# Fetching a block's neighbour lists by node in layer 0 of a two-layer graph attention kernel

## The chip, the core and the metric

The kernel runs on one core of a Trainium2 chip. The metric is the device time of one execution in microseconds. A core has five engines that each work through their own queue of instructions in order: TensorE (PE, matrix products), VectorE (DVE), ScalarE (ACT), GpSimd (POOL) and SyncE (SP). They wait for each other by semaphores. Transfers between the chip's memory and the on-chip buffer are done by 16 DMA engines. An indirect transfer, a gather of rows by a list of row numbers, is issued by POOL.

## What is computed

A graph of 2708 nodes goes through two layers of attention. Each node has 1024 features, and `adj` says which pairs are neighbours; a node has a few to 40 of them. The reference, cut to what matters:

```python
def layer0(x, adj):
    f = x @ Wf + bf
    g = x @ Wg + bg
    e = relu(f @ g.T)
    attention = softmax(where(adj > 0, e, -9e15), axis=1)
    return attention @ (x @ W + bW)

def layer1(x, adj):
    h = x @ W1
    e = leaky_relu(h @ a1 + (h @ a2).T, 0.2)
    attention = softmax(where(adj > 0, e, -9e15), axis=1)
    return relu(attention @ h)

x = layernorm(x + layer0(x, adj))
x = layernorm(x + layer1(x, adj))
```

## The kernel before

The kernel does not work on the 2708 x 2708 matrix. A prelude reads `adj` once and makes of each row a list of its neighbours' numbers, 40 places long (`CAP`), which goes to `LD` in the chip's memory (`keep_lists`, line 625). A list is stored as 4 runs of 10 places (`QT`), place t of run q being neighbour 4t + q. Nodes are then sorted by the length of their lists and cut into 85 groups of 32 nodes; four groups make a block of 128 rows, and there are 22 blocks (one of them has a single group).

A group is worked on as a set of tiles. A tile has 128 partitions: partition 32q + i stands for node i of the group, and holds one neighbour of that node, the t-th of run q. So the lists of a group are needed as a 128 x 10 piece of the buffer `SL`, whose partition 32q + i holds run q of node i. `SL` (line 152) is one tile of 128 x 85 x 10 integers for all groups. `load_lists(b)` (line 1065) fetches them: for each of the block's 4 groups it issues one gather of 128 short rows (10 integers, 40 bytes) out of `LD`, by the row numbers `idq`, straight into the group's piece of `SL`. Another table, `ids`, holds the number of the node in each of a block's 128 rows.

Layer 0 is a loop over the 22 blocks (the loop that calls `lay.sums` at line 1279). One round k, for block u, does in this order:

- `lay.sums` (line 920): PE multiplies the softmax weights of block u into the neighbours' rows of `x`, which lie in the `ring`, a buffer of 20 tiles of 128 rows with 4 KB each. Each time both halves of a tile are used up, its place is free, and `gathers` (line 877) issues on POOL the gather of the next tile into it: 128 rows of `x`, 512 KB, by one column of `SL`. A block has 20 tiles in most rounds, so these are the tiles of the next block.
- POOL's queue then gets: the scatter of the finished block before to `T1` (in `close`, line 1139), the gather of a later block's own rows (`load_x`, line 1087), the gather of the residual rows into `z` (`load_residual`, line 1133), and `load_lists` for the block four rounds on (line 1316). Rounds 1 to 17 have such a call.
- PE makes the two dense products of the round (f for the block two rounds on, the output product of the block before), ACT copies f to the partitions of the tiles (`replicate`).
- `dots` (line 1123): DVE makes one dot product per tile of the next block, as soon as that tile has landed. `soft` (line 1128) makes the softmax weights of the next block. The norm of the block before follows (`close`).

The class `InOrder` keeps each engine's instructions in the order in which the program issues them. The waits are put in by the recording layer, from what each instruction reads and writes. Each of POOL's DMAs adds 16 to one of eight semaphores, taken in turn, when all of its data has landed, and a DMA waits until the one before it on its semaphore has landed, eight DMAs back.

Layer 1 works on the same lists, all of which are in `SL` by then, and gathers from `T1`. All engine calls go through a helper, so every operation of both layers has the line number 71 in the profile.

Of the kernel before, what the change touches and what calls it, by code (L numbers as in the profile page):

```python
# [10 lines left out]
I32 = mybir.dt.int32  # L11
# [23 lines left out]
CAP = 40  # L35
# [71 lines left out]
def listed_path(ctx, tc, x, adj, Wf, bf, Wg, bg, W, bW, W1, a1, a2, out):  # L107

    nc = tc.nc
    P = 128  # L110
# [8 lines left out]
    nrows = [32] + [P] * (NB - 1)  # L119
    valid = [N - 32 * (NG - 1)] + [P] * (NB - 1)  # L120
    start = [0] + [valid[0] + P * b for b in range(NB - 1)]
    groups = [[0]] + [list(range(g, g + 4)) for g in range(1, NG, 4)]
    QT = CAP // 4
    Q = 4
# [8 lines left out]
    pe, dve, act, pool, sp = (InOrder(tc, e) for e in (nc.tensor, nc.vector, nc.scalar, nc.gpsimd, nc.sync))  # L133
# [8 lines left out]
    LD = dram.tile([N * Q, QT], I32, name="LD")  # L142
# [9 lines left out]
    SL = const.tile([P, NG, QT], I32, name="SL")  # L152
    SL0 = const.tile([P, NSL0, QT], I32, name="SL0")
    ids = const.tile([P, NB], I32, name="ids")
# [28 lines left out]
    def gather(engine, dst, table, idx, rows=N):  # L183
        engine.indirect_dma_start(
            out=dst, out_offset=None, in_=table,
            in_offset=bass.IndirectOffsetOnAxis(ap=idx, axis=0), bounds_check=rows - 1, oob_is_err=False)
# [33 lines left out]
    with ExitStack() as prelude:  # L220
        new_pool = lambda name, bufs: prelude.enter_context(tc.tile_pool(name=name, bufs=bufs))
# [476 lines left out]
        t = adjp.tile([P, N], F32, name="adj")  # L698
# [6 lines left out]
        b = full - 1  # L705
# [136 lines left out]
    def cut(most, turns, order):  # L842


        units, at = [], 0
        for i, b in enumerate(order):
            u = Unit()
            u.b, u.gs, u.at = b, groups[b], at
            u.G, u.T, u.n = len(u.gs), max(TILES[g] for g in u.gs), nrows[b]
            u.tiles = [(k, g, t) for k, g in enumerate(u.gs) for t in range(TILES[g])]  # L850
            u.col = {(k, t): m for m, (k, g, t) in enumerate(u.tiles)}
            u.tiles.sort(key=lambda m: (m[0] // turns, m[2]))
            u.sc = scores[i % 2][:, :u.G, :u.T]
            assert len(u.tiles) <= min(most, MOST)
            at += len(u.tiles)
            units.append(u)
        return units

    class Layer:
# [3 lines left out]
        def __init__(self, units, rings, width, table, stp):  # L863
            self.units, self.table, self.width, self.stp = units, table, width, stp

            self.first = {g: i for i, g in enumerate(g for u in units for g in u.gs)}
            self.slots = [(t, i) for t in rings for i in range(t.shape[1])]
            self.count = len(self.slots)
            self.order = [(u, g, t) for u in units for _, g, t in u.tiles]
            assert all(self.first[g] < NSL0 for _, g, _ in self.order[:self.count])  # L870
            self.next, self.free, self.most = 0, set(), len(self.order)

        def rows(self, m):
            t, k = self.slots[m % self.count]
            return t[:, k, :self.width]

        def gathers(self, latest=None):
            ready = []
            while self.next < min(self.most, len(self.order)) and (self.next < self.count or self.next - self.count in self.free):
                ready.append(self.next)  # L880
                self.next += 1
            if latest is not None and latest + self.count in ready:
                ready.remove(latest + self.count)
                ready.insert(0, latest + self.count)
            for m in ready:
                u, g, t = self.order[m]
                idx = SL[:, g, t:t + 1] if m >= self.count else SL0[:, self.first[g], t:t + 1]
                gather(pool, self.rows(m), self.table, idx)

        def soft(self, u):  # L890

# [173 lines left out]
    def load_lists(b):  # L1065
        for g in groups[b]:
            gather(pool, SL[:, g, :], LD[:, :], idq[:, g:g + 1], N * Q)

    def spread(v, n, name):

        qd = small.tile([P, Q], F32, name=name)
        dve.tensor_scalar(qd[:n], quad[:n], v, None, op0=ALU.mult)
        return qd
# [3 lines left out]
    with s0s:  # L1077
        new_pool = lambda name, bufs: s0s.enter_context(tc.tile_pool(name=name, bufs=bufs))
        tp, frp = new_pool("tp", 2), new_pool("frp", Q)
        stp, xp, yp, jp = (new_pool(n, 1) for n in ("stp0", "xp", "yp", "jp0"))  # L1080
        zs = new_pool("zp", 1).tile([P, TW], F32, name="z")
        seq = [1, 0, *range(2, NB)]
        units = cut(R0, 2, seq)
        lay = Layer(units, [ring], D, x, stp)
        xb, q, qd, F, Fr, xTs, yTs, Wp, y, Z = ({} for _ in range(10))
# [23 lines left out]
        def x_turn(b):  # L1109
            xTs[b] = tp.tile([P, KC, P], F32, name="xT")  # L1110
            for _ in turn(xb[b], nrows[b], xTs[b]):
                pass
# [4 lines left out]
        def replicate(b, k):  # L1117

            Fr[b, k] = frp.tile([P, D], F32, name="Fr")
            for p in range(Q):  # L1120
                act.copy(Fr[b, k][32 * p:32 * p + 32, :], flat(F[b])[32 * k:32 * k + 32, :])
# [130 lines left out]
        for k, u in enumerate(units):  # L1252
            nxt = units[k + 1] if k + 1 < len(units) else None
            b = u.b
            back = seq[k - 1] if k > 0 else None
            ahead = seq[k + 2] if k + 2 < NB else None

            first = k == 0
            po = ps_s.tile([P, H, 512], F32, name="po")
            y[b] = yp.tile([P, D], F32, name="y")  # L1260
            if back is not None:
                for _ in yTs[back][1]:
                    pass
            reps = list(range(len(nxt.gs))) if nxt is not None and not first else []
            for r in reps[:1]:
                replicate(nxt.b, r)
            next(closing, None)
            if loaded is not None:
                q_dot(loaded)
                loaded = None  # L1270
            next(closing, None)
            for r in reps[1:3]:
                replicate(nxt.b, r)
            if nxt is None:

                for _ in closing:
                    pass
                Wp[back] = product(P, yTs.pop(back)[0], Wt, 1)
            lay.sums(u, po, y[b])
            if first:  # L1280
                u_rows()
            for _ in closing:
                pass
            closing = iter(())
            if ahead is not None and not first:
                x_turn(ahead)
            if k + 3 < NB and not first:
                loaded = seq[k + 3]
                load_x(loaded)
            if back is not None and nxt is not None:  # L1290
                load_residual(back)
                if back > 0:
                    Wp[back] = product(P, yTs.pop(back)[0], Wt, 1)
                else:
                    Wp[back] = whole(split_product(yTs.pop(back)[0], Wt, frp.tile([P, D], F32, name="Fr"), 1))
            if k + 2 == NB:
                load_residual(b)
            spreading = iter(())
            if ahead is not None and not first:
                spreading = q_spread(ahead)  # L1300
                next(spreading)
            for r in reps[3:]:
                replicate(nxt.b, r)
            if ahead is not None and not first:
                f_product(ahead)
            if ahead == NB - 1:
                sp.dma_start(M, W1.rearrange("(k p) d -> p k d", p=P))
            yT = tp.tile([P, KC, P], F32, name="xT")
            steps = turn(y[b], nrows[b], yT, halves=True)
            next(steps)  # L1310
            yTs[b] = yT, steps
            if k + 2 == NB:
                for _ in steps:
                    pass
            if k + 4 < NB and not first:
                load_lists(seq[k + 4])
            if nxt is not None:
                dots(nxt, 0, len(nxt.tiles))
            for _ in spreading:
                pass  # L1320
            if nxt is not None:
                soft(nxt)
            if back is not None:
                closing = close(back)
                next(closing)
        b = NB - 1
# [10 lines left out]
    with ExitStack() as s1s:  # L1337
        new_pool = lambda name, bufs: s1s.enter_context(tc.tile_pool(name=name, bufs=bufs))
# [11 lines left out]
        lay = Halves(units, [ring, more], TW, T1[:, :], stp)  # L1350
        done1 = {b: i for i, b in enumerate(order1)}
        for u in units:
            g, at = u.gs[0], lay.first[u.gs[0]]
# [90 lines left out]
        for n, (u, ks) in enumerate(parts):  # L1444
            b, po = u.b, banks[:, n % 2, :]
# [7 lines left out]
            if turning is not None:  # L1453
                v, kv, _ = turning
# [11 lines left out]
            if ks[-1] + 1 == u.G:  # L1466
                k = done1[b]
# [387 lines left out]
```

## Time and profile before

| | |
|---|---|
| median of 9 runs | 1715.17 us (1712.06 to 1718.64) |
| the profiled execution | 1716.65 us; its span 1714.9 us, so 1.75 us lie around the span |
| busy in the span | PE 1540.4 us (90%), DVE 1291.9 (75%), ACT 631.3 (37%), POOL 1159.6 (68%) |
| the loop of layer 0 | about 240 to 1050 us after the span's start |
| gathers of tiles in layer 0 | 405, mean 1069 ns each on POOL |
| gathers of lists | 85, mean 1022 ns each on POOL; 68 of them in the loop, in 17 rounds |
| one round, scatter to `T1` to scatter to `T1` | 41.0 us, mean of the 15 from 319.25 to 934.42 us |

The busy time of a gather on POOL is the time in which POOL issues it. The data lands later; that is read from the start of the instruction that waits for it. Two gathers that follow each other directly start 1.29 us apart, 0.99 us of issuing and 0.30 us between. "Idle before" in a row is how long the engine stood still, and the arrow names what the profile takes to have ended that.

### The profile page before, as it was taken

Reading aid. Unit: us, or ns where it says so; the run is one execution under the profiler, and the core shown is the slowest. Engines: PE = TensorE matmul, PEld = TensorE weight load, DVE = VectorE, ACT = ScalarE, POOL = GpSimd, SP = SyncE. Lnnn points to the kernel's source line nnn. Section 1 sums busy time; section 2 is a strip of 40 time slices with the busy share of each in tenths; the row PEclk is TensorE's granted clock in tenths of the full one; section 3 lists DMA queues with packets and bytes.
Section 4 is the critical chain, followed back from the end, with each engine's and each line's share of the span. In section 5 each row is a group of like instructions: output and inputs, shape, how many; then the busy total and the mean of one; then the engine's idle time right before and its main releaser. Section 6 shows DMA issues by size and latency. Waiting matters only on the chain. (4 is left out here: it accounts for less than half of the span.)

```text
span 1714.9 us, 22758 instructions
## 1 busy us (share of the span) xinstructions
PE 1540.4 (90%) x6851; PEld 664.2 (39%) x6873; DVE 1291.9 (75%) x4158; ACT 631.3 (37%) x886; POOL 1159.6 (68%) x1130
## 2 busy tenths in 40 slices
PE   6996779899999999999999999379998988999896
PEld 3542333343444444444444444123333433334332
DVE  6998668898999988999999788456566555665662
ACT  6671425554554544444444554011111111111111
POOL 7994674667676766777667644377777777777740
PEclk9998989999999999999999999789999999999998
DMA  8772584777887877888877766599999999999961
GB/s 339 295 258 115 195 310 146 271 252 274 297 298 282 285 271 286 296 289 295 299 277 265 280 232 260 179 396 367 370 371 396 391 390 374 386 394 391 391 253 38
DMA packets 150961, 503.95 MB, mean 294 GB/s; under 512 B 32714, under 2 KB 32730, under 8 KB 148398
## 3 DMA queue, kind: packets, MB, share of 16 engines
q0 software_dynamic: 131648, 428.27, 67.7%
q1 hardware_dynamic: 16128, 73.71, 11.3%
q8 instruction: 56, 0.92, 0.2%
q10 hardware_dynamic: 3054, 0.43, 0.1%
q14 instruction: 75, 0.61, 0.1%
HBM read 510.81 MB, written 33.75 MB: 318 GB/s over the span
## 5 line engine op out<-in xcount | busy, mean ns | idle before, releaser
L71 POOL DMA_INDIRECT ring<-in_x_dram,SL x405 | 432.8, 1069 | 159.0 <-issue 76.2
L71 DVE SCALAR_TENSOR_TENSOR j<-ring,Fr 128x1024 bf16<-128x1024 f32 x402 | 493.2, 1227 | 54.9 <-ACT Fr L71 23.7
L71 PE MATMUL po<-ring,st 128*32 128x512 f32 x2616 | 330.0, 623 | 58.5 <-DVE st L71 28.0
L71 ACT COPY Fr<-pm 32x1024 f32<-32x1024 f32 (+2 forms) x353 | 340.6, 965 | 6.9 <-PE pm L71 2.1
L71 PE MATMUL pm<-M,yT 128*128 128x512 f32 (+1 forms) x704 | 313.3, 598 | 0.5 <-ACT yT L71 0.5
L71 POOL DMA_INDIRECT ring<-T,SL x249 | 246.9, 992 | 81.3 <-issue 66.2
L71 PE MATMUL pm<-Wt,xT 128*128 128x512 f32 (+1 forms) x704 | 297.0, 594 | 0.1
L71 PE MATMUL pm<-M,xT 128*128 128x512 f32 x672 | 295.0, 597 | 0.3 <-issue 0.2
L71 ACT ACTIVATE scores<-scores 128x12 f32<-128x12 f32 (+9 forms) x65 | 14.0, 216 | 641.9 <-DVE scores L71 641.9
L71 PEld LDWEIGHTS pm<-M,yT 128*128 128x128 f32 (+1 forms) x704 | 127.8, 186 | 184.7 <-issue 183.5
L71 PEld LDWEIGHTS pm<-Wt,xT 128*128 128x128 f32 (+1 forms) x704 | 129.6, 187 | 156.1 <-issue 152.2
L71 PEld LDWEIGHTS pm<-M,xT 128*128 128x128 f32 x672 | 128.9, 192 | 155.6 <-issue 152.6
L71 POOL DMA_INDIRECT more<-T,SL x156 | 154.6, 991 | 47.9 <-issue 42.5
L71 PEld LDWEIGHTS po<-ring,st 128*32 128x32 f32 x2616 | 95.5, 114 | 234.1 <-issue 160.7
L71 POOL TENSOR_TENSOR adj<-adj,iota 128x2708 f32<-128x2708 f32 (+2 forms) x23 | 124.5, 5458 | 11.6 <-ACT adj L71 11.6
L71 PE MATMUL pm<-halfT,Wt 128*128 128x512 f32 x256 | 118.9, 620 | 0.0
L71 DVE MAX8 cand<-adj 128x8 f32<-128x170 f32 x336 | 95.6, 321 | 17.9 <-POOL adj L71 17.9
L71 POOL DMA_INDIRECT SL<-LD,idq x85 | 86.8, 1022 | 28.1 <-issue 24.2
L71 PE MATMUL po<-more,st 128*32 128x512 f32 x624 | 86.6, 648 | 13.9 <-ACT y L71 13.9
L71 DVE TENSOR_SCALAR scores<-ring,f1q 128x4 f32<-128x4 f32 (+6 forms) x69 | 16.0, 238 | 94.3 <-DMA ring<-T,SL 71.4
L71 POOL DMA_INDIRECT z<-in_x_dram,ids x21 | 23.3, 1109 | 88.5 <-issue 31.9
L71 PEld LDWEIGHTS pm<-halfT,Wt 128*128 128x128 f32 x256 | 49.9, 200 | 59.2 <-issue 59.1
(236 smaller groups left out, 1466.7 us busy)
## 6 DMA issues: line engine op xcount, KB each, us to landing
adj<-in_adj_dram SPq DMA_DIRECT2D x19, 1354.0 KB, 7.0
X1S<-z SPq DMA_DIRECT2D x19, 512.0 KB, 5.9
ring<-in_x_dram,SL POOLq DMA_INDIRECT x405
rows<-in_L_gnn_Wg_dram SPq DMA_DIRECT2D x8, 512.0 KB
rows<-in_L_gnn_Wf_dram SPq DMA_DIRECT2D x8, 512.0 KB
M<-in_L_gnn_W_dram SPq DMA_DIRECT2D x1, 4096.0 KB
ring<-T,SL POOLq DMA_INDIRECT x249
u1b<-X1S SPq DMA_DIRECT2D x7, 512.0 KB, 4.9
```

The lines of the kernel that those rows point to most:

```text
L71: made = self.tc.keep_in_program_order(op(*args, **kwargs))
```

## The change

`load_lists` stays for the first blocks. In rounds 1 to 17 the call at line 1316 is replaced. `load_rows` issues one gather: for each of the block's 128 rows the whole list of its node (40 integers, 160 bytes), by `ids`, into a new tile `nodes` (two buffers). Partition 32k + i now holds all four runs of node i of group k. `place_rows` then copies 16 pieces of 32 x 10 integers on POOL, run q of group k to partitions 32q to 32q + 31 of the group's place in `SL`. It is a generator that does one copy at each step. `gathers` steps it once after each gather that it issues, so in the next round one copy stands in POOL's queue behind each of the first 16 gathers of tiles. What is left of it is done before the next `load_rows`.

```diff
             self.next, self.free, self.most = 0, set(), len(self.order)
+            self.between = iter(())
...
                 gather(pool, self.rows(m), self.table, idx)
+                next(self.between, None)
...
+    def load_rows(b, nodes):
+        t = nodes.tile([P, CAP], I32, name="nodes")
+        gather(pool, t[:nrows[b]], LD.rearrange("(n q) t -> n (q t)", q=Q), ids[:nrows[b], b:b + 1])
+        return t
+
+    def place_rows(b, t):
+        for k, g in enumerate(groups[b]):
+            for q in range(Q):
+                pool.tensor_copy(SL[32 * q:32 * q + 32, g, :], t[32 * k:32 * k + 32, q * QT:(q + 1) * QT])
+                yield
...
+        nodes = new_pool("nodes", 2)
...
+            for _ in lay.between:
+                pass
             if k + 4 < NB and not first:
-                load_lists(seq[k + 4])
+                lay.between = place_rows(seq[k + 4], load_rows(seq[k + 4], nodes))
```

## The prediction

> **What bounds the kernel now.** I read the busy time by stretches first, for four rounds of layer 0. The columns are the stretch, its length, then busy microseconds (and instructions) of PE, PE's weight loads, DVE, ACT and POOL, PE's granted clock, the DMA engines' share and GB/s.
>
> ```profile
> 575.00:616.00 41.00, 40.75 (x186) 17.74 (x186) 37.67 (x86) 20.76 (x25) 28.35 (x27) 1.00 0.78 271
> 616.00:658.00 42.00, 40.01 (x184) 17.44 (x184) 37.20 (x84) 20.77 (x25) 28.83 (x28) 1.00 0.76 270
> ```
>
> A round is full on PE (40.8 of 41 us) and nearly on DVE (37.7). POOL shows 28.4, but with the 0.30 us between gathers its 27 instructions take 27 x 1.29 = 35 us. All three are close to the bound. So little can be won here, and much be lost on any one of them. The timeline of POOL for the round from 607.93 us shows the rest (start, length, instruction, idle before):
>
> ```profile
> 607.93 1.02 POOL L71 DMA_INDIRECT T<-z,ids  x1 [0.30 <-DVE j L71]
> 609.25 1.03 POOL L71 DMA_INDIRECT xb<-in_x_dram,ids  x1 [0.30 <-issue]
> 615.15 0.99 POOL L71 DMA_INDIRECT z<-in_x_dram,ids  x1 [4.87 <-DVE scores L71]
> 616.45 1.00 POOL L71 DMA_INDIRECT SL<-LD,idq  x1 [0.30 <-issue]
> 617.75 1.21 POOL L71 DMA_INDIRECT SL<-LD,idq  x1 [0.30 <-issue]
> 619.26 1.00 POOL L71 DMA_INDIRECT SL<-LD,idq  x1 [0.30 <-issue]
> 620.57 0.99 POOL L71 DMA_INDIRECT SL<-LD,idq  x1 [0.30 <-issue]
> 621.87 1.00 POOL L71 DMA_INDIRECT ring<-in_x_dram,SL  x1 [0.30 <-issue]
> 623.17 0.99 POOL L71 DMA_INDIRECT ring<-in_x_dram,SL  x1 [0.30 <-DVE rstd L71]
> ...
> 648.13 0.99 POOL L71 DMA_INDIRECT ring<-in_x_dram,SL  x1 [0.30 <-issue]
> 649.42 1.01 POOL L71 DMA_INDIRECT T<-z,ids  x1 [0.30 <-issue]
> ```
>
> The 20 gathers of tiles take 27.55 us (621.87 to 649.42), one each 1.29 us or a little more, because none waits for the landing of the one before. The other part, scatter to first gather, takes 13.94. How long a gather of 512 KB takes to land is seen where DVE waits for `z` and finds the DMA queue otherwise short:
>
> ```profile
> 619.52 1.23 DVE L71 TENSOR_TENSOR z<-pm,z 128x1024 f32<-128x1024 f32 x1 [1.01 <-DMA z<-in_x_dram,ids]
> ```
>
> It was issued by 615.15 + 0.99 = 616.14 and used at 619.52: 3.38 us. Read in the same way, eight other rounds give 3.29 to 3.51. In the full stream it is longer: the fifth tile's gather ended at 628.76 and its dot product waited until 635.38, 6.6 us.
>
> **The change part by part.** *Removed:* three of the four list gathers, 3 x 1.30 = 3.9 us of POOL's queue in each of 17 rounds. They stand between `z` and the first tile, so the first tile can go 3.9 us earlier, if PE has a place free.
>
> *Added:* 16 copies of 32 x 10 integers on POOL per round. No row shows such a copy. The nearest are a POOL memset of 20 x 7 (104 ns) and the one POOL copy, 128 x 1 (371 ns); after a memset the next gather came 0.15 us later, after a gather 0.30. So copy and gap cost between 0.25 and 0.67 us, and I take 0.45, the middle, since its neighbours on both sides are equally far. The new tile costs nothing but buffer space. The one list gather left moves 128 rows of 160 bytes in place of 512 of 40, which only relieves the DMA queue.
>
> *Moved, and this decides:* a copy stands behind a gather, and it waits. I read the waits in the list of the changed program's instructions. In all 17 rounds it is the same. The first copy waits for the list gather. The second to fourth wait for no DMA. The fifth waits for everything POOL has issued up to then, tile gathers 1 to 5 with it, and each of the copies 6 to 16 waits for the semaphore value that the tile gather directly before it leaves: for its landing. Gathers 6 to 17 wait in turn for the copy before them. The cells of `SL` in question are not the same (the gathers read the next block's columns, the copies write a block three on), so it is an order that the data do not need, but the chip will keep it. So gathers 5 to 16 no longer stream. Each must land before the next is issued: 12 landings per round, 204 in all. Behind the waiting copy stand all later tile gathers, the scatter to `T1`, `xb` and `z`; DVE's dots and through them PE's sums wait for those.
>
> One such step is 0.99 (issue) + 3.37 (landing, the rows above, which fit since the queue now is short) + 0.45 = 4.81 us in place of 1.29. From the start of the 17th gather of one round to that of the next:
>
> - gathers 17 to 20, which have no copies: issued by 4.87, the last landed at 8.24;
> - its dot product, 1.27 from one to the next: 9.5; `soft` until PE starts its sums: 859.62 to 863.66 and 614.36 to 618.14 in two rounds, 3.9: 13.4; PE's first four matmuls, 0.46, and the semaphore: first place free at 14.0. POOL has its other work done at about 13.8 (scatter from 5.2, its landing some 5 us after 6.2 as at 568.61 to 573.87, then `z` and one list gather), so this is even;
> - four gathers with free copies, 4 x 1.45 = 5.8, and 0.5 for the first copy, whose list gather was issued just before: 20.3;
> - 12 steps of 4.81, 57.7: 78.0 us.
>
> Against 41.0 us this is +37.0 per round, and over 17 rounds +629. PE's dense work (28 us a round) and DVE's other work lie inside the 78 us and cost nothing; without this cover they would be the 41 us of now. Should PE's clock sag because it idles half the time (it shows 0.72 for 1100 to 1150 us, with PE 53% busy), only the 0.46 us before the first free place are on the path: 0.2 x 17 = 3 us. Nothing outside the loop changes. The sum is made against the profiled execution: 1716.65 + 629 = 2346, and as that execution lies 1.5 us above the median, 2345.
>
> Bounds of the step: 0.99 + 3.29 + 0.25 = 4.53 and 0.99 + 3.51 + 0.67 = 5.17. With the four free gathers at 1.25 and 1.66 and 0.2 to 1 for the first copy, the round is 73.6 or 83.7, the time 1715 + 17 x 32.6 = 2269 or 1715 + 17 x 42.7 = 2441.
>
> The Trainium skill prices a landing too ("DMA: Bandwidth & Descriptors", section "Anatomy of one DMA — SWDGE (gpsimd) path"): about 2.0 us plus bytes over 436 GB/s, nearly all of the fixed part being completion, which only a chain of dependent DMAs pays each time. For 512 KB that is 3.20 us, against the 3.38 of the row; by it the sum would be 204 x 0.17 = 35 us less, about 2310. It speaks against the change by the same mechanism.
>
> **The rivals.** *The landings cost what they cost in the full stream.* If the 6.6 us of the fifth tile's row were the latency of a scattered gather and not its queue, a step would be 8.04: 1715 + 17 x (37.0 + 12 x 3.23) = 3003. Against it: `z` is a gather of the same table by equally scattered rows, and lands in 3.3 to 3.5. Chance 0.04.
>
> *The waits are met early and only the copies count.* POOL's round gets 16 x 0.45 - 3.9 = 3.3 us longer, and as the tiles feed DVE at 1.29 against 1.27 us, DVE follows: 1715 + 17 x 3.3 = 1771. For it speaks only that the profile cannot show a wait that is not yet there. Against it: the value waited for is the one that the gather just issued leaves. Chance 0.05.
>
> *The change does what its words say, and it is faster.* Then the copies hide in the 0.30 us between gathers, tiles start up to 3.9 us earlier, and DVE's waits for tiles and for `z` between 350 and 1000 us go: 14.2 + 13.4 us, 1715 - 28 = 1687; more is not to be had, as PE is 40.8 us busy in 41. It decides if a step costs under about 1.29 + 3.9/16 = 1.53 us. Chance 0.03, for the same reason.
>
> **How the numbers follow.** The serial landings get 0.88, at 2345, the likeliest. Its own bounds are 2269 to 2441; I widen them to 2230 to 2490, since a landing among other traffic (the store of a block to memory, once a round) may be longer and one whose lists have empty places shorter than the `z` rows. That leaves 0.12 for the rivals and some 0.07 of the main case outside. No change within 0.2% (3.4 us, about what a measurement of this kernel can tell) could only come by chance between the rivals: 0.01. Faster 0.03, slower 0.96.
>
> **What would show it.** Right: POOL rows in the loop in which a copy has some 3.4 us of idle before it, released by the tile's DMA, 12 times a round; tile gathers 4.5 to 5.2 us apart; rounds of 74 to 84 us; PE and DVE about half idle from 290 to 1600 us; layer 1 as long as before. Wrong in size: a landing far from 3.4 us. Wrong altogether: tile gathers still 1.3 to 1.6 us apart.

## The result, and the profile after

| | before | after |
|---|---|---|
| median | 1715.60 us of 31 runs | 2590.02 us of 10 runs (2582.96 to 2593.79) |
| ratio to before | | 1.5088 (95% interval 1.5068 to 1.5108) |
| span of the profiled execution | 1714.9 us | 2588.1 us |
| first list gather of the loop to the first gather of layer 1 | 267.42 to 1100.97: 833.6 us | 264.89 to 1968.32: 1703.4 us |
| mean period, first tile gather to first tile gather, 16 periods | 40.9 us | 92.1 us (86.4 to 94.3) |

The kernel takes half as long again as before, 245 us more than the 2345 that were forecast and 100 us above the range. 870 of the 873 us that the span grew by lie in the loop of layer 0; what comes before it is 2.5 us shorter and layer 1 with the end 5.9 us longer.

The busy time by stretches, for two rounds after the change (stretch, length, busy microseconds and instructions of PE, weight loads, DVE, ACT and POOL, PE's granted clock, DMA share, GB/s):

```profile
833.00:926.00 93.00, 41.00 (x181) 17.51 (x182) 36.82 (x81) 20.75 (x25) 30.71 (x40) 0.72 0.40 126
926.00:1016.00 90.00, 42.54 (x183) 17.78 (x182) 37.68 (x86) 20.77 (x25) 32.30 (x41) 0.73 0.39 123
```

A round does the work that it did before: PE 41 to 42.5 us, DVE 37 to 38, ACT 20.8. It only takes 90 us for it. No engine is full, and the DMA engines move half as much per second: the time is waiting. Where it waits is in POOL's timeline after the change (start, length, instruction, idle before and what ended it), from the first tile gather of a round:

```profile
930.97 0.99 POOL L71 DMA_INDIRECT ring<-in_x_dram,SL  x1 [2.90 <-PE po L71]
932.01 0.18 POOL L71 COPY SL<-nodes 32x10 int32<-32x10 int32 x1
932.35 1.01 POOL L71 DMA_INDIRECT ring<-in_x_dram,SL  x1 [0.16 <-issue]
...
936.70 0.36 POOL L71 COPY SL<-nodes 32x10 int32<-32x10 int32 x1
937.22 1.02 POOL L71 DMA_INDIRECT ring<-in_x_dram,SL  x1 [0.16 <-issue]
944.77 0.31 POOL L71 COPY SL<-nodes 32x10 int32<-32x10 int32 x1 [6.54 <-issue]
945.62 1.58 POOL L71 DMA_INDIRECT ring<-in_x_dram,SL  x1 [0.54 <-POOL SL L71]
950.52 0.18 POOL L71 COPY SL<-nodes 32x10 int32<-32x10 int32 x1 [3.33 <-DMA ring<-in_x_dram,SL]
951.35 1.33 POOL L71 DMA_INDIRECT ring<-in_x_dram,SL  x1 [0.64 <-POOL SL L71]
955.89 0.19 POOL L71 COPY SL<-nodes 32x10 int32<-32x10 int32 x1 [3.21 <-DMA ring<-in_x_dram,SL]
```

Four copies are free: 0.18 us each (0.36 the fourth), the next gather mostly 0.16 us behind. The fifth stands 6.54 us until the five gathers before it have landed (by the program's list of waits; the arrow names no releaser). From the sixth on every copy waits for the tile gather just before it, 3.2 us in the mean of all rounds (183 of 187 between 2.7 and 4.0, four 1.2), and the gather behind it waits another 0.64 us for the copy ("POOL SL"). So from here gathers come 5.4 us apart where they came 1.3 apart. The page's groups of the changed kernel say the same in sums (busy, mean ns of one, then idle before and what ended most of it):

```profile
L71 DVE SCALAR_TENSOR_TENSOR j<-ring,Fr 128x1024 bf16<-128x1024 f32 x402 | 492.7, 1226 | 913.5 <-DMA ring<-in_x_dram,SL 886.2
L71 POOL DMA_INDIRECT ring<-in_x_dram,SL x405 | 492.2, 1215 | 276.3 <-POOL SL L71 121.6
L71 POOL COPY SL<-nodes 32x10 int32<-32x10 int32 x272 | 71.4, 262 | 701.4 <-DMA ring<-in_x_dram,SL 606.4
```

The copies stand 701 us, and DVE's dots 914 us, nearly all of it for tiles. The issue of a tile gather, which before took 1069 ns in the mean, now takes 1215.

### The profile page after: what moved, and what is told of

The parts are those of the page before. It is cut to its first block, busy times and chain, and to the rows that moved or that the text cites. A ratio compares the mean times of both kernels' runs of the same rounds, so it can differ in the third digit from the quotient of the medians.

```text
span 2588.1 us, 22892 instructions
## 1 busy us (share of the span) xinstructions
PE 1584.1 (61%) x6851; PEld 674.9 (26%) x6873; DVE 1293.7 (50%) x4158; ACT 631.4 (24%) x886; POOL 1249.5 (48%) x1351
## 5 line engine op out<-in xcount | busy, mean ns | idle before, releaser
L71 POOL DMA_INDIRECT ring<-in_x_dram,SL x405 | 492.2, 1215 | 276.3 <-POOL SL L71 121.6
L71 PE MATMUL pt<-ident,y 128*128 128x128 f32 (+1 forms) x360 | 61.0, 302 | 790.4 <-DVE q L71 789.3
L71 PE MATMUL po<-ring,st 128*32 128x512 f32 x2616 | 363.2, 679 | 95.4 <-DVE st L71 64.1
L71 POOL COPY SL<-nodes 32x10 int32<-32x10 int32 x272 | 71.4, 262 | 701.4 <-DMA ring<-in_x_dram,SL 606.4
L71 PEld LDWEIGHTS pt<-ident,y 128*128 128x128 f32 (+1 forms) x360 | 46.7, 155 | 830.6 <-DVE q L71 793.3
```

The costliest lines, as they stand in the source:

```text
L71: made = self.tc.keep_in_program_order(op(*args, **kwargs))
```

## The experiments

The ratios are to the kernel before, run on the same chip; its median there was 1715.96 us for the first four kernels and 1718.75 for the others. "Landing" is counted from the end of a gather's issue to the start of what waits for it.

**1. The copies on ScalarE.** Is it the fetching by node, or the copies on POOL, that cost?

```diff
-pool.tensor_copy(SL[32 * q:32 * q + 32, g, :], t[32 * k:32 * k + 32, q * QT:(q + 1) * QT])
+act.copy(SL[32 * q:32 * q + 32, g, :], t[32 * k:32 * k + 32, q * QT:(q + 1) * QT])
```

> The 16 copies of a round are made by ScalarE in place of GpSimd; the one list gather by node stays. In the program's list no copy waits for a tile gather any more. Theory (the waits of GpSimd's copies for the landings cost everything): tile gathers 1.29 us apart again, a round of 39 to 41 us, 1690 to 1725 us in all. Rival A (fetching by node itself, or the copies' later arrival, is what costs): well above 1800 us. Rival B (the freed 3.9 us of GpSimd's queue per round are worth something): 1687 to 1705 us; if they are worth nothing, because TensorE is full in 40.8 of 41 us, 1710 to 1720 us.

Measured: 1717.20 us, ratio 1.0007 (0.9994 to 1.002), no landing waited for between tile gathers. The tile gathers' group, first of the kernel before, then of this one:

```profile
L71 POOL DMA_INDIRECT ring<-in_x_dram,SL x405 | 432.8, 1069 | 159.0 <-issue 76.2
```

```profile
L71 POOL DMA_INDIRECT ring<-in_x_dram,SL x405 | 431.4, 1065 | 225.4 <-PE po L71 96.7
```

The idle time before the tile gathers grew by 66.4 us, which is 17 x 3.9: the three list gathers saved per round came back as idle time, most of it waiting for a free place in PE's ring ("PE po", 43.2 us before, 96.7 now). In 17 rounds of this kernel the first tile gather starts 1.35 us after the first product of PE's sums, when the first place comes free. So fetching by node costs nothing and wins nothing here, and the 874 us belong to the copies' place on POOL.

**2. The waits taken away, the copies left on POOL.** In the list of waits of the built program a POOL copy waits for tile gathers only where its source begins at partition 32 or above; one that reads partitions 0 to 31 waits for the list gather alone. Here all copies read the first group's lists, so the other groups work with wrong neighbours, and the count of lists that are too long is left out.

```diff
-t[32 * k:32 * k + 32, q * QT:(q + 1) * QT]
+t[:32, q * QT:(q + 1) * QT]
...
-                    pool.memset(over[:, g, TILES[g]:], 1.0)
+                    pool.memset(over[:, g, TILES[g]:], 0.0)
```

> GpSimd makes all 16 copies at the same places of its queue, but each reads partitions 0 to 31 of the fetched lists, so all groups of a block work with the first group's lists, and the count of lists that are too long is left out. In the program's list only the first copy waits, for the list gather. Theory (waits, not copies): 1690 to 1745 us; a copy costs 0.1 to 0.3 us between two gathers, as behind gathers 1 to 4 of the changed kernel, 1.6 to 4.8 us per round against the 3.9 saved. Rival (GpSimd's copies between its gathers disturb each other, waits or not: longer issue, contention with VectorE): 2000 us or more.

Measured: 1886.21 us, ratio 1.0983 (1.096 to 1.1006). The waits are gone and with them 704 of the 874 us, but 170 us stay, which neither theory had. POOL's timeline of this kernel shows what they are:

```profile
554.25 1.96 POOL L71 DMA_INDIRECT ring<-in_x_dram,SL  x1 [0.16 <-DVE j L71]
...
559.54 0.82 POOL L71 COPY SL<-nodes 32x10 int32<-32x10 int32 x1
...
563.07 0.18 POOL L71 COPY SL<-nodes 32x10 int32<-32x10 int32 x1
563.41 1.02 POOL L71 DMA_INDIRECT ring<-in_x_dram,SL  x1 [0.16 <-issue]
```

and DVE's, in the same stretch:

```profile
554.09 1.23 DVE L71 SCALAR_TENSOR_TENSOR j<-ring,Fr 128x1024 bf16<-128x1024 f32 x1
555.36 1.23 DVE L71 SCALAR_TENSOR_TENSOR j<-ring,Fr 128x1024 bf16<-128x1024 f32 x1
...
559.09 1.23 DVE L71 SCALAR_TENSOR_TENSOR j<-ring,Fr 128x1024 bf16<-128x1024 f32 x1 [0.81 <-DMA ring<-in_x_dram,SL]
```

The copy at 559.54 starts inside a dot and ends at 560.36, with the dot (559.09 + 1.23 = 560.32); the copy at 563.07 meets none and takes 0.18. The issue at 554.25 starts inside a dot that runs to 555.32 and takes 1.96 us. Between 440 and 900 us the 38 copies that meet no dot take 0.18 us, the 110 that meet one 0.50 in the mean and up to 1.28; issues take 1.01 without (48) and 1.46 with a dot (136). So a second cost was there: DVE's dots hold POOL up, while their own length stays 1.23 us. The trace gives the rule. Each of the 184 copies of the run that start inside a dot ends 0.04 to 0.06 us after that dot. Each of the 143 tile gathers' issues that start inside a dot, past its first 0.05 us and with more than 0.17 us of it left, ends 0.86 to 0.90 us after the dot; the others take 0.98 to 1.10 us.

**3. Four copies behind each of the first four gathers.** If the time goes by the number of landings waited for, three per round instead of twelve should take three quarters of it away.

```diff
-                next(self.between, None)
+                for _ in range(4):
+                    next(self.between, None)
```

> Four copies stand behind each of the first four tile gathers, in place of one behind each of 16. In the program's list three copies per round wait for landings in place of 12; the number of copies is the same. Theory (each landing costs some 4.2 us more than a streamed gather): 9 landings less per round, 9 x 4.2 x 17 = 640 us below the changed kernel, 1880 to 1980 us. Rival (the copies themselves cost): 2590 us, as before.

Measured: 2044.50 us, ratio 1.1914 (1.1886 to 1.1942). The nine landings fewer in 17 rounds give (2590.02 - 2044.50) / 153 = 3.57 us each, near one landing, though less than a whole step. It is above what was expected. In POOL's timeline of this kernel, the first bundles of one round:

```profile
648.33 0.86 POOL L71 COPY SL<-nodes 32x10 int32<-32x10 int32 x4
...
654.21 3.22 POOL L71 COPY SL<-nodes 32x10 int32<-32x10 int32 x4 [3.85 <-DMA ring<-in_x_dram,SL]
657.70 1.87 POOL L71 DMA_INDIRECT ring<-in_x_dram,SL  x1 [0.27 <-POOL SL L71]
662.86 1.76 POOL L71 COPY SL<-nodes 32x10 int32<-32x10 int32 x4 [3.29 <-DMA ring<-in_x_dram,SL]
```

The landings are like those of the changed kernel, but four copies that take 0.86 us alone take 3.22 and 1.76 beside DVE's dots: the same contention, in a new place.

**4. All copies together at the end of the round**, ahead of the next list gather.

```diff
-                next(self.between, None)
```

> The 16 copies stand together at the end of the next round, before the next list gather, none between the tile gathers. One wait per round, for the landing of the residual rows (3.4 us after their issue), then 16 copies and a list gather, some 8.7 us from residual gather to first tile gather in place of 5.2. Theory: +3 to +4 us per round, 1740 to 1800 us. Rival (as copies hide there: TensorE bounds the round anyway): 1710 to 1725 us.

Measured: 1759.16 us, ratio 1.0267 (1.0236 to 1.0298), as expected. One wait is left per round, and the copies keep their own length. POOL's timeline of this kernel:

```profile
498.91 0.88 POOL L71 COPY SL<-nodes 32x10 int32<-32x10 int32 x4
502.49 2.69 POOL L71 COPY SL<-nodes 32x10 int32<-32x10 int32 x12 [2.69 <-issue]
```

That is 0.22 us a copy with the gap behind it: of DVE's operations there, the short ones of `soft`, the sum `z<-pm,z` with PE's output and the statistics of `z`, none is a dot of two tiles in the buffer. The sum is as long as a dot (1.22 us) and has two inputs, but one is PE's output; the 71 copies that start inside it take 0.18 to 0.19 us. (1759.16 - 1715.96) / 17 = 2.5 us per round remain.

**5. Experiments 2 and 3 together:** no waits, and the copies early in the round, where they were thought to meet no dots.

```diff
-t[32 * k:32 * k + 32, q * QT:(q + 1) * QT]
+t[:32, q * QT:(q + 1) * QT]
...
-                next(self.between, None)
+                for _ in range(4):
+                    next(self.between, None)
...
-                    pool.memset(over[:, g, TILES[g]:], 1.0)
+                    pool.memset(over[:, g, TILES[g]:], 0.0)
```

> As the run in which all copies read partitions 0 to 31 (first group's lists for all groups, no count of long lists, no wait for tile gathers), but four copies stand behind each of the first four tile gathers, while VectorE is still at the norm and its dot products have hardly begun. Theory (a GpSimd copy or issue that meets a dot product of VectorE stands until that ends; without one a copy takes 0.18 us): most of the 170 us go, 1715 to 1775 us. Rival (each GpSimd copy between gathers costs, wherever it stands): 1886 us again.

Measured: 1874.63 us, ratio 1.0907 (1.0886 to 1.0928). The thought was wrong: DVE's products of the finished block and the first dots run there too, the first four gathers take 12 to 14 us instead of 6, and the gathers behind them, now out of step with the dots, are issued more slowly (1.23 us in the mean, against 1.07 in the kernel before). The time alone does not tell the theories apart.

**6. The cause of the contention: dots with one input.** The dot product reads two tiles. Here it is a sum over one of them with the same shape and nearly the same length (1220 ns), in the changed kernel, in experiment 2 (there with the count left out as well), and in the kernel before as a control.

```diff
-dot(lay.rows(u.at + m), Fr[u.b, k], P, u.sc[:, k, t:t + 1])
+dve.tensor_scalar(jp.tile([P, D], BF16, name="j"), lay.rows(u.at + m), 1.0, 0.0, op0=ALU.mult, op1=ALU.add, accum_out=u.sc[:, k, t:t + 1])
```

In the kernel after the change:

> The changed kernel with its 12 landings per round, but each of VectorE's dot products over a tile is replaced by a sum over one input (the scores are row sums, so the output is another). Theory (the step was 5.43 and not 4.81 us because the dot of the tile that has just landed starts together with the copy, and holds GpSimd up): the gap behind a copy falls from 0.64 to about 0.3 us, the issue from 1.33 to 1.0, the step to 4.7 to 4.9, 204 x 0.6 = 120 to 150 us less, 2430 to 2480 us. Rival (the gap and the longer issue belong to a gather that waits for the copy's own semaphore): 2590 us, gap and issue as before.

Measured: 2515.16 us, ratio 1.4639 (1.4597 to 1.4681). POOL's timeline:

```profile
917.46 0.18 POOL L71 COPY SL<-nodes 32x10 int32<-32x10 int32 x1 [3.27 <-DMA ring<-in_x_dram,SL]
918.28 1.01 POOL L71 DMA_INDIRECT ring<-in_x_dram,SL  x1 [0.64 <-POOL SL L71]
```

The issue fell from 1.33 to 1.01 us: that part of the step was contention. The 0.64 us between copy and gather stayed: that part is the wait for the copy itself. The time lies between the two ranges: each theory was right about one part.

In experiment 2:

> The run in which all copies read partitions 0 to 31, 1886 us, with the sum over one input in place of the dot product. Theory (contention with two-input work of VectorE made the 170 us): copies 0.18 to 0.2 us also where VectorE is busy, tile gathers 1.35 us apart, 1690 to 1750 us. Rival: 1886 us.

In the kernel before:

> The kernel before with the same replacement of the dot product, as the control of the two others. If the dots are not what bounds a round (TensorE full in 40.8 of 41 us): 1695 to 1720 us. If the tile gathers' issue was held up by dots before too (21 of 195 issues over 1.25 us), a little of that goes, 5 to 15 us.

Measured: 1726.91 us, ratio 1.0048 (1.0033 to 1.0063), and for the control 1701.02, ratio 0.9902 (0.9884 to 0.9921). The groups of the tile gathers and of the copies in experiment 2, then in this form of it:

```profile
L71 POOL DMA_INDIRECT ring<-in_x_dram,SL x405 | 524.6, 1295 | 172.4 <-PE po L71 85.5
L71 POOL COPY SL<-nodes 32x10 int32<-32x10 int32 x272 | 118.4, 435 | 12.2
```

```profile
L71 POOL DMA_INDIRECT ring<-in_x_dram,SL x405 | 429.0, 1059 | 161.2 <-PE po L71 61.3
L71 POOL COPY SL<-nodes 32x10 int32<-32x10 int32 x272 | 59.1, 217 | 12.2
```

Against its own control the copying costs 1726.91 - 1701.02 = 26 us where DVE's operation has one input, and 170 us where it has two. So 144 of the 170 us of experiment 2 are contention with a DVE operation that reads two tiles. The copies' busy time fell by 59 us and the issues' by 96.

## Why the prediction was wrong in size

**What held.** The waits are where the prediction put them: four copies free, then twelve landings per round, in all 17 rounds. Experiment 1 shows that they come from the copies on POOL, experiments 2 and 3 that most of the time goes with their number. The landing itself was forecast as 3.37 us and measured as 3.24 (mean of the 187 waits of the sixth to sixteenth copies; median 3.29). PE's and DVE's work is hidden, as said. The prediction named a landing far from 3.4 us as the sign of a wrong size; the landing was the term that came out right.

**What failed** is the sizing of the round, from 17th gather to 17th gather: 78.0 us by the prediction, 92.0 measured (mean of 16), 14.0 more, and 17 x 14.0 = 238 of the 245 us. By its own steps:

| step of the prediction | forecast | measured | difference per round |
|---|---|---|---|
| four free gathers and the first copy | 6.3 | 6.8 | 0.5 |
| the first of the twelve waits | 4.81 | 8.2 | 3.4 |
| the other eleven steps | 11 x 4.81 | 11 x 5.43 | 6.8 |
| 17th gather to the next first | 14.0 | 17.2 | 3.2 |

*"One such step is 0.99 (issue) + 3.37 (landing, ...) + 0.45 = 4.81 us"*, the 0.45 for copy and gap. Measured are 1.35 + 3.24 + 0.84 = 5.43. Both other terms were too small: copy and gap lie above their bound of 0.67, and the issue got no bounds at all; 0.99 was taken as fixed. But the landing that lets the copy go also starts the dot of that tile on DVE, so the next issue meets that dot: 178 of the 187 issues start inside one, and 175 take over 1.25 us. DVE's timeline of the changed kernel shows it for the copy of 950.52 and the gather of 951.35 above:

```profile
950.56 1.23 DVE L71 SCALAR_TENSOR_TENSOR j<-ring,Fr 128x1024 bf16<-128x1024 f32 x1 [4.25 <-DMA ring<-in_x_dram,SL]
```

The dot runs to 951.79, the issue starts at 951.35 and takes 1.33, so it ends 0.89 us after the dot, by the rule of experiment 2. From 440 to 900 us in the changed kernel, 57 of the 74 issues that meet a dot take over 1.25 us. In the kernel before only 21 of 195 do: gathers 1.29 us apart and dots 1.27 apart ran nearly in step, and 205 of the 290 issues that start inside a dot do so in its last 0.17 us, where it no longer holds them up. The trace of the kernel before has issues of 1.7 to 1.96 us in the loop; the prediction left them out of the sum. The one-input sum in the changed kernel (experiment 6) confirms the size: it is 75 us faster, and in its trace the eleven steps take 5.10 us in place of 5.43 and the first wait 7.7 in place of 8.2, which is 17 x (11 x 0.33 + 0.5) = 70 us.

The Trainium skill has a rule for this, "SBUF — State Buffer", section "SBUF: two separate sides": VectorE and GpSimd share a pair of ports that one instruction holds as a whole, a VectorE operation with two inputs in the buffer against a GpSimd operation that reads it. The runs agree: in experiment 2 every copy that started inside a dot ended with it, and with a one-input operation in the dot's place the copies' mean fell from 435 to 217 ns.

*"Copy and gap cost between 0.25 and 0.67 us, and I take 0.45."* The copy was shorter than taken (0.185), the gap longer (0.66). The nearest rows were those of a gather behind an instruction that it need not wait for, 0.15 to 0.30. The prediction itself says that gathers 6 to 17 wait for the copy before them, and gave that wait no price. The first four copies, whose gathers do not wait, keep 0.16.

*The first wait* was priced like the others, but five gathers are in flight there, and the landing took 5.4 us in the mean. The fifth gather's issue (1.5 us) and the copy with its gap (1.3) are longer too, as dots of the first tiles run beside them. The prediction had quoted 6.6 us for the fifth tile of a full stream and priced only a rival with it.

*"First place free at 14.0"*. In the round whose 17th gather starts at 1003.37 the last tile's dot starts at 1013.42, 1.8 us later than forecast: its landing took 4.8 us, with four gathers in flight. PE then starts at 1018.39, and the next gather at 1020.61, 2.22 us on, where 0.6 were forecast. PE's timeline of the changed kernel with the busy time of the same stretch (PE's granted clock is the third number from the end), and like rows of the kernel before:

```profile
1018.39 3.64 PE L71 MATMUL po<-ring,st 128*32 128x512 f32 x16 [2.43 <-DVE st L71]
1018.40:1022.00 3.60, 3.60 (x31) 0.97 (x34) 2.66 (x5) 3.56 (x6) 1.18 (x3) 0.50 0.17 65
```

```profile
863.66 1.92 PE L71 MATMUL po<-ring,st 128*32 128x512 f32 x16
863.66:865.58 1.92, 1.92 (x37) 0.72 (x40) 1.59 (x3) 1.91 (x5) 1.62 (x2) 1.00 0.07 6
```

After 45 us without work, and but four short products since, PE does 16 products in 3.64 us at a granted clock of 0.50, before in 1.92 at 1.00; and eight of them must be done before a place is free, not four: eight have ended when the gather starts, here as in experiment 1. There, at the full clock, the gather follows 1.35 us after PE's start. So of the 1.6 us per round 0.75 are the wrong count and 0.87 the sag of the clock, 17 x 0.87 = 15 us where the prediction had 3. The Trainium skill, "TensorE: Matmul & The Clock Gate", section "Part 1: The HAM clock gate", says that an idle array runs at half rate until it has been busy for some 3.4 us, which agrees with the 0.50 granted over 3.6 us in these rows.

**The rivals.** Landings at full-stream latency (3003 us) fell: 3.24 us with one gather in flight; only where several are in flight was it longer (5.4 us for the first wait). *Only the copies count* (1771) was wrong about the waits, and experiment 2, which makes its condition true, shows 1886: without any wait the copies still cost 170 us, since its price had no contention in it. *Faster* (1687) fell in experiment 1: with no waits and 3.9 us less in POOL's queue the time is that of before, as PE's ring has no free place earlier.

**What stays open.** Why the recording layer orders a POOL copy whose source begins above partition 31 behind all POOL's transfers was not found; reversing the order of the copies, another target and another kind of POOL operation all kept the 12 waits per round in the built programs. A version with these copies on POOL, with the right sources and without the waits, was not tried. No version ran faster than the kernel before with the same computation; the copies on ScalarE are level with it.

## What to carry to other kernels

A small instruction put into a queue of streamed transfers is priced by what it waits for and by what then waits for it, not by its length: 0.18 us of copying made a step of 1.3 us into one of 5.4. When a stream is made serial, go through every term of the step again, since what ran in step before (POOL's issues and DVE's dots) then meets each time, and what was kept warm or overlapped (PE's clock, queued landings) is paid in full. Before giving work to POOL, look whether DVE is running operations with two inputs in the buffer at that time.

## What the runs showed of the hardware that was not expected

- The issue of a gather on POOL, not only a POOL copy, is held up by a DVE operation with two inputs in the buffer: 1.01 us without one, 1.46 us in the mean with one, up to 2.06 us (experiment 2, 184 issues). An issue that starts after the dot's first 0.05 us and before its last 0.17 ends 0.86 to 0.90 us after the dot (82 issues in the kernel before, 216 in the changed one, 143 in experiment 2); of the other 774 issues of these runs one took over 1.10 us. A DVE operation as long with one input in PE's output does not hold a copy (0.18 to 0.19 us, 71 copies of experiment 4). With the one-input sum in the changed kernel the issues in the steps are 1.01 to 1.02 us.
- This contention is in the kernel before too: with the one-input sum its tile gathers' issue falls from 1069 to 1024 ns and its time by 1.0% (0.9884 to 0.9921).
- A gather that has to wait for a copy just before it on its own engine starts 0.64 us after it, one that does not 0.16 us after it.
